# Chunk transposes by DVE blocks and SBUF transfers, second norm on ACT, in a gated recurrence with a binary FFN

## The chip, the cores and the metric

The kernel runs on one core of a Trainium2 chip. The core has five engines that run side by side, each through its own queue in order: PE (matrix products), DVE (element-wise work and statistics), ACT (activation functions), POOL (a slower element-wise engine) and SP, which here only issues DMA transfers. They meet through semaphores. The metric is the device time of the program in microseconds (us).

## The reference

The input x has 2 sequences of 4096 tokens with 256 features. A gated linear recurrence with a tanh state of 64 runs over the tokens, its result is projected and added to x, and a LayerNorm follows; then an FFN with weights reduced to a sign and a scale per row, exact Gelu, hidden width 1024, and a second LayerNorm:

```
u = x @ W_in + b_in
g = sigmoid(x @ W_gate + b_gate)
h_t = tanh(h_prev @ A + u_t @ Bm)
y_t = h_t @ C.T + u_t @ D.T
y_t = g_t * y_t + (1.0 - g_t) * x_t
x   = layernorm(x + (ys @ W_out + b_out + x))
h   = gelu(x @ binarize(w1).T + b1)
x   = layernorm(x + (h @ binarize(w2).T + b2))
```

Everything is float32. Where one operand of a product is a sign, the other is written as a sum of two parts in a faster product format (`fp32r`): `hi`, the rounded value, and `lo`, the rest. Two products give nearly the float32 result.

## The kernel before

**Tiles.** The sequences are cut into 64 segments each, which the recurrence advances together, 128 columns a step (with a warm-up that makes the segments independent). The rest of the work goes by 16 chunks of 512 tokens. A chunk lives in two layouts: tokens on partitions (`x1`, a tile `xn` of 128 partitions x 4 blocks x 256 features) for the norms, and features on partitions (`hi`/`lo`, named `xhi`/`xlo`, 128 x 2 x 512) as the input of the first FFN product.

**A chunk's way.** `load` fetches the states and inputs of the recurrence (`hu`) and the rows of x (`xn`). `mix` makes y's first term on PE (`ps_y`) and `d` on DVE; `mix_end` applies the gate (two DVE operations, L382 and L385). `project` multiplies by W_out on PE (`ps_z`), adds the residual on DVE (L406) and starts the first norm's statistics (`bs_a`, `mv_a`, `rs_a`; the power is taken on POOL). `shift` and `norm` apply that norm on ACT (`nm_a`, then four activations, L279). `turn` transposes x1 with eight PE transposes into PSUM (`ps_t`, L423), makes `xhi` on ACT (L431) and `xlo` on DVE (L433). `rest` adds the row b2 on POOL (L355). Four groups g of `up`, `low` and `down` do the FFN: `up` multiplies (`ps_h`, L451), applies Gelu twice on ACT (L458) and rounds (`hhi`, L467); `low` makes `hlo` on DVE (L474); `down` multiplies by w2 (`ps_o`, L490), and after its last group `scale` takes the sum out of PSUM (`o`, L506). `add` adds the residual (L512), `stats` starts the second norm (`bs_b`, `mv_b`, `rs_b`), and `store` applies it, on DVE unless told otherwise (four operations, L281; on ACT it first makes `nm_b` on DVE, L271), and writes the chunk out on SP's queue.

**Order.** PE, ACT, DVE and POOL follow an order written out by hand: the order in which the Python code calls the pieces is the order of each engine's queue. SP's queue is ordered by the scheduler. In the main loop, iteration c works on several chunks at once: `up`, `low`, `down` 0 and 1 of chunk c, `down` 2 and 3, `add`, `stats` and `store` of chunk c - 1, `norm` and `turn` of chunk c + 1, `mix` and `project` of chunk c + 2. `step` puts one step of the recurrence between them (`ps_s` on PE, a tanh on ACT, L158) as long as any are left, and gate products (`ps_g`, L313) of a late chunk go in as well. So one iteration of the loop before is, in order:

```
up 0, low 0, step, down 2 (c-1), load (c+3), shift, norm (c+1), mix (c+2)
up 1, step, down 3 (c-1), add, stats (c-1), gate
turn (c+1), low 1, rest (c+1)
up 2, low 2, store (c-1), step, down 0, project 0 (c+2)
up 3, step, down 1, low 3, project 1 (c+2)
```

**Buffers.** `d` and `o` each have one buffer of 4 KB a partition, `xhi` and `xlo` two each. In PSUM the tag "m" (one buffer of two banks) serves `ps_y`, `ps_z` and `ps_t` in turn, and three single banks serve `ps_h` and `ps_g`.

Of the kernel before, what the change touches and what calls it, by code (L numbers as in the profile page):

```python
# [8 lines left out]
FP = mybir.dt.float32  # L9
FR = mybir.dt.float32r  # L10
# [6 lines left out]
P = 128  # L17
B, T, DM, S, H = 2, 4096, 256, 64, 1024
KD = DM // P
# [4 lines left out]
N = 512  # L24
# [3 lines left out]
TB = N // P  # L28
# [9 lines left out]
def gated_recurrence_then_binary_ffn(  # L38
# [16 lines left out]
    nc = tc.nc  # L55
# [3 lines left out]
    wk = ctx.enter_context(tc.tile_pool(name="work", bufs=2))  # L59
# [269 lines left out]
    class Chunk:  # L329


        def __init__(self, c, name, at=lambda a, c: a[c]):
            self.c, self.nm, self.at, self.xt = c, name, at, None

        def load_x(self):
            self.xt = xp.tile([P, KD, N], FP, tag="xt", name=f"xt_{self.nm}", bufs=XTB)
# [28 lines left out]
        def mix(self):  # L365

            nm, xt_ = self.nm, self.xt
            ps = p_m.tile([P, KD, N], FP, tag="m", name=f"ps_y{nm}")
            for m in range(KD):
                nc.tensor.matmul(  # L370
                    ps[:, m, :], cd[:, bass.ts(m, P)], self.hu, start=True, stop=True
                )
                if m < KD - 1:
                    yield
            self.add_row(self.xn, bo_r)
            self.d = wk.tile([P, KD, N], FP, tag="y", name=f"d{nm}", bufs=1)
            nc.vector.tensor_sub(self.d, ps, xt_)
            yield

# [38 lines left out]
        def turn(self, apart=False):  # L418
# [15 lines left out]
            self.h = {}  # L434
            yield

        def rest(self):

            self.add_row(self.x1, b2_r)
            yield  # L440

        def up(self, g, apart=False):
            nm = f"{self.nm}_{g}"
            h = wk.tile([P, 2, N], FP, tag="h", name=f"h{nm}")
            hi = wk.tile([P, 2, N], FR, tag="hhi", name=f"hhi{nm}", bufs=3)
            self.h[g] = h, hi
            for i in range(2):
                j = 2 * g + i
                ps = p_1.tile([P, N], FP, tag="h", name=f"ps_h{nm}_{i}")
                for n, (k, part) in enumerate((k, p) for p in (self.hi, self.lo) for k in range(KD)):  # L450
                    nc.tensor.matmul(  # L451
                        ps,
                        sg1[:, k, bass.ts(j, P)],
                        part[:, k, :],
                        start=n == 0,
                        stop=n == 2 * KD - 1,
                    )
                nc.scalar.activation(  # L458
                    h[:, i, :],
                    ps,  # L460
                    AF.Gelu,
                    bias=b1_c[:, j : j + 1],
                    scale=al1[:, j : j + 1],
                )
                if i == 1:
                    for part in range(2) if apart else [slice(0, 2)]:
                        nc.scalar.copy(hi[:, part, :], h[:, part, :])  # L467
                yield
# [167 lines left out]
    def do(i, what, *args, pace=5600):  # L636
        if not 0 <= i < len(ch):
            return
        if what == "load":
            need = WARM + (ch[i].c + 1) * SPC  # L640
            while done < need:
                next_steps()
            ch[i].load()
        elif what in ("load_x", "load_gate_x"):
            getattr(ch[i], what)()
        else:
            emit(what, getattr(ch[i], what)(*args), pace)
# [7 lines left out]
    with tc.manual_schedule(engines={ET.PE, ET.Activation, ET.DVE, ET.Pool}):  # L655
        waiting = []
        for c in range(FIRST + 1, FIRST + 6):
            load_xT(c)
        idle_products(7)
        emit("u", u_of_chunks(FIRST), 1 << 30)  # L660
        since = 0
        pairs = [(5, 6), (7, 8), (9, 10), (11, 12), (13, 14), (), (1, 2)]
        loads = [[10, 11], [12, 13], [14, 15, 0], [1, 2], [3], [], []]
        for n, pair in enumerate(pairs):
            before = 2 if n == 0 else 1
            parts(before, EARLY)
            if pair:
                emit("", u_of_chunks(*pair))
                if pair == (13, 14):
                    emit("", u_of_chunks(15, 0))  # L670
                emit("u", [None], EARLY)
            for c in loads[n]:
                load_xT(c)
            if n == 0:
                load_weights()
            if n == 3:
                halve_weights()
            if n >= 5:
                load_xT(n + 3)
            for i in range(7 - before):  # L680
                if 1 <= n < 5 and i == 0:
                    load_w(n - 1)
                if 2 <= n < 6 and i == 3:
                    prepare_w(n - 2)
                parts(1 if (n, i) != (6, 5) else 0, EARLY)
        assert done >= WARM + SPC, done
        emit("u", u_of_chunks(3), EARLY)
        for i in range(4):
            ch[i].xt = x_tiles[i]
        do(0, "mix", pace=850)  # L690
        do(0, "mix_end")
        parts(1, 600)
        assert done >= WARM + 2 * SPC, done
        do(1, "mix", pace=850)
        do(1, "mix_end")
        parts(1, 600)
        do(0, "project", 0, p_2, "o", pace=1700)
        do(0, "project", 1, pace=1700)
        assert done >= WARM + 3 * SPC, done
        do(2, "mix", pace=1700)  # L700
        do(0, "shift")
        do(1, "project", 0, p_2, "o", pace=1700)
        do(0, "norm")
        do(1, "project", 1, pace=1700)
        mixed = ch[2].mix_end()
        next(mixed)
        parts(2, 1700)
        while waiting:
            next_steps()
        waiting = None  # L710
        do(0, "turn", True)
        emit("", mean_w2())
        do(1, "norm", nc.vector)
        do(0, "rest")
        next(mixed)
        parts(2, 1700)
        for i in (4, 5):
            do(i, "load_x")
        end = len(ch) - 1
        parts_met = compare()  # L720
        since = -1 << 40
        late = gates(ch[10:], TB)
        for c in range(end):
            do(c + 6, "load_x")
            if c % 2 == 0:
                do(10 + c // 2, "load_gate_x")
            do(c, "up", 0)
            do(c, "low", 0)
            step()
            do(c - 1, "down", 2)  # L730
            do(c + 3, "load")
            if c > 0:
                do(c + 1, "shift")
                do(c + 1, "norm")
                do(c + 2, "mix")
                do(c + 2, "mix_end")
            do(c, "up", 1)
            step()
            do(c - 1, "down", 3)
            def add():  # L740
                do(c - 1, "add", range(TB), nc.gpsimd if c == end - 1 else nc.vector)
                if c < end - 1:
                    do(c - 1, "stats")

            if 1 <= c <= 12:
                add()
                emit("gate", (next(late, None) for _ in range(KD)))
            do(c + 1, "turn")
            do(c, "low", 1)
            if not 1 <= c <= 12:  # L750
                add()
            do(c + 1, "rest")
            do(c, "up", 2)
            do(c, "low", 2)
            if c == end - 1:
                do(c - 1, "stats")
            else:
                do(c - 1, "store")
            if c == end - 2:
                assert done == len(plan), done  # L760
                next(parts_met)
                next(parts_met)
            step()
            do(c, "down", 0)
            do(c + 2, "project", 0)
            do(c, "up", 3)
            step()
            do(c, "down", 1)
            do(c, "low", 3)
            if c == end - 1:  # L770
                do(c - 1, "store")
            do(c + 2, "project", 1)
            if c == end - 2:
                next(parts_met)
                next(parts_met)
        count()
        do(end, "up", 0)
        do(end, "low", 0)
        do(end - 1, "down", 2)
        do(end - 1, "down", 3)  # L780
        do(end, "up", 1)
        do(end - 1, "add")
        do(end - 1, "stats")
        do(end, "low", 1)
        do(end, "up", 2)
        do(end, "low", 2)
        do(end, "down", 0, True)
        do(end, "up", 3, True)
        do(end - 1, "store", range(TB), nc.scalar)
        do(end, "low", 3, True)  # L790
        do(end, "down", 1)
        do(end, "down_end")
# [64 lines left out]
```

## Time and profile before

| What | Value |
|---|---|
| Median of the runs | 451.27 us |
| Lowest and highest of three runs | 451.14 and 453.04 us |
| The profiled execution | 451.76 us, of it a span of 450.0 us |
| Transposes on PE, `ps_t` | 128 of 0.274 us each |
| `xlo` from PSUM on DVE | 15 of 1.219 us (and two halves) |
| The second norm on DVE, L281 | 58 of 0.695 us, four to a chunk |
| The first norm on ACT, L279 | 60 of 0.591 us, four to a chunk |
| `hu`, the transfers from SBUF to SBUF | 32 of 128 KB, 2.2 us from issue to landing |

The span is the time from the first to the last instruction that the profile shows. Mean durations of pipelined instructions overlap: eight transposes of 0.274 us take less than eight times that. The up products of the first iteration begin at 87.2 us, those of the last chunk end some 15 us before the span's end; the iterations between are nearly equal, and what is read of one of them holds for the others.

### The profile page before, as it was taken

How to read it: one execution, taken by the hardware profiler on the slowest of the kernel's cores; microseconds unless marked ns; L12 is line 12 of the kernel's file. 1: busy time of each engine (PE TensorE's matmuls, PEld its weight loads, DVE VectorE, ACT ScalarE, POOL GpSimd, SP SyncE). 2: the span in 40 equal slices, each digit the busy share in tenths (PEclk: the TensorE clock that was granted, in tenths of full speed). 3: DMA queues.
4: the chain of work that ended last, by engine and by line, in shares of the span. 5: the costliest groups of instructions: out<-in, count | busy, mean ns of one | idle time of the engine just before them, and what ended most of it. 6: DMA issues, size and time to landing. Idle time of an engine off the chain costs nothing.

```text
span 450.0 us, 6729 instructions
## 1 busy us (share of the span) xinstructions
PE 438.2 (97%) x2506; PEld 355.6 (79%) x2506; DVE 357.4 (79%) x597; ACT 259.9 (58%) x424; POOL 177.6 (39%) x177
## 2 busy tenths in 40 slices
PE   8999999999999999999999999999999999999992
PEld 5665766788888888887979797979788888897982
DVE  0245927967979797989898889899898989887774
ACT  2443541585656574847474747566666656565771
POOL 1001300643545454545445454545454545433413
PEclk9999999999999999999999999999999999999997
DMA  8997824221133313331331313111202020201013
GB/s 298 306 320 289 290 67 134 69 86 23 48 108 104 108 58 106 105 106 58 105 106 61 105 60 105 61 58 50 70 20 87 1 93 1 93 1 48 1 47 101
DMA packets 14838, 44.51 MB, mean 99 GB/s; under 512 B 2000, under 2 KB 3024, under 8 KB 14800
## 3 DMA queue, kind: packets, MB, share of 16 engines
q1 hardware_dynamic: 14224, 43.65, 29.2%
q8 instruction: 22, 0.36, 0.4%
q10 hardware_dynamic: 576, 0.37, 0.3%
q14 instruction: 16, 0.13, 0.1%
HBM read 31.43 MB, written 8.39 MB: 88 GB/s over the span
## 4 chain that ended last, share of the span: by engine, by line
PE 86%; DVE 6%; DMA 3%; ACT 3%; issue 1%; POOL 1%; SPq 0%; POOLq 0%; DVEq 0%
PE ps_h L451 24%; PE ps_o L490 23%; PE ps_z L395 12%; PE ps_g L313 11%; PE ps_y L370 6%; PE ps_s L157 5%; PE ps_u L131 3%; PE ps_t L423 3%; DMA xt<-in_xT 3%; DVE hlo L474 1%; ACT xn L279 1%; ACT h L458 1%; DVE xn L281 1%; DVE bs_a L256 1%; ACT hhi L467 1%
## 5 line engine op out<-in xcount | busy, mean ns | idle before, releaser
L458 ACT ACTIVATE h<-ps_h,bias_c,al 128x512 f32<-128x512 f32 x128 | 97.4, 776 | 86.3 <-PE ps_h L451 80.3
L490 PE MATMUL ps_o<-sg,hhi 128*128 128x256 f32 x496 | 121.3, 285 | 0.0
L490 PE MATMUL ps_o<-sg,hlo 128*128 128x256 f32 x496 | 117.9, 279 | 0.1
L474 DVE TENSOR_TENSOR hlo<-h,hhi 128x1024 fp32r<-128x1024 f32 (+1 forms) x65 | 83.7, 1305 | 23.1 <-ACT hhi L467 23.0
L490 PEld LDWEIGHTS ps_o<-sg,hlo 128*128 128x128 f32 x496 | 93.5, 188 | 1.1 <-DVE hlo L474 0.3
L490 PEld LDWEIGHTS ps_o<-sg,hhi 128*128 128x128 f32 x496 | 93.5, 189 | 0.8
L451 PE MATMUL ps_h<-xhi,sg 128*128 128x512 f32 x256 | 91.8, 440 | 0.0
L355 POOL TENSOR_TENSOR xn<-xn,bo_r 128x256 f32<-128x256 f32 x64 | 65.4, 1052 | 48.4 <-DMA xn<-in_x 48.4
L451 PE MATMUL ps_h<-xlo,sg 128*128 128x512 f32 x256 | 80.1, 394 | 0.2
L355 POOL TENSOR_TENSOR xn<-xn,b_r 128x256 f32<-128x256 f32 x64 | 70.8, 1134 | 2.0 <-PE ps_t L423 2.0
L467 ACT CAST hhi<-h 128x1024 fp32r<-128x1024 f32 (+1 forms) x65 | 67.3, 1037 | 2.0
L313 PE MATMUL ps_g<-xt,w_gate 128*128 128x384 f32 (+3 forms) x208 | 66.3, 430 | 0.2 <-DMA xt<-in_xT 0.2
L266 POOL TENSOR_TENSOR rs_a<-rs_a,neg_half 128x4 f32<-128x4 f32 x16 | 17.2, 1075 | 121.3 <-DVE rs_a L265 96.6
L395 PE MATMUL ps_z<-w_out,tg 128*128 128x256 f32 x256 | 60.7, 380 | 0.0
L158 ACT ACTIVATE st<-ps_s 64x128 f32<-64x128 f32 x112 | 30.1, 269 | 47.6 <-PE ps_s L157 47.1
L451 PEld LDWEIGHTS ps_h<-xlo,sg 128*128 128x128 f32 x256 | 48.1, 188 | 11.8 <-DVE xlo L433 0.9
L451 PEld LDWEIGHTS ps_h<-xhi,sg 128*128 128x128 f32 x256 | 46.6, 189 | 13.4 <-issue 6.2
L157 PEld LDWEIGHTS ps_s<-st,wab 128*128 128x128 f32 x224 | 38.5, 188 | 22.2 <-ACT st L158 10.0
L266 POOL TENSOR_TENSOR rs_b<-rs_b,neg_half 128x4 f32<-128x4 f32 (+1 forms) x17 | 19.2, 1132 | 87.9 <-PE ps_s L157 49.9
L395 PEld LDWEIGHTS ps_z<-w_out,tg 128*128 128x128 f32 x256 | 46.1, 189 | 5.1
L279 ACT ACTIVATE xn<-xn,nm_a,rs_a 128x256 f32<-128x256 f32 x60 | 31.2, 591 | 26.5 <-DVE nm_a L271 26.5
L157 PE MATMUL ps_s<-st,wab 128*128 128x128 f32 x224 | 43.9, 278 | 0.1
(73 smaller groups left out, 483.5 us busy)
## 6 DMA issues: line engine op xcount, KB each, us to landing
xt<-in_xT SPq DMA_DIRECT2D x35, 512.0 KB, 4.2
xn<-in_x SPq DMA_DIRECT2D x16, 512.0 KB, 3.4
out_y<-xn SPq DMA_DIRECT2D x15, 512.0 KB, 2.6
hu<-st SPq DMA_DIRECT2D x32, 128.0 KB, 2.2
w1t<-in_w1T SPq DMA_DIRECT2D x2, 512.0 KB, 5.6
w1n<-in_w SPq DMA_DIRECT2D x2, 512.0 KB, 6.3
w2t<-in_w2T SPq DMA_DIRECT2D x2, 512.0 KB, 4.7
xt<-in_xT SPq DMA_DIRECT2D x2, 256.0 KB, 3.4
```

The source lines that it names most:

```text
L157: nc.tensor.matmul(p_h, ab, st[:, j].rearrange("p b k -> p (b k)"), start=True, stop=True)
L158: nc.scalar.activation(h_of[:, j + 1].rearrange("p b k -> p (b k)"), p_h[TOP, :], AF.Tanh)
L266: nc.gpsimd.tensor_tensor(rs, rs, neg_half[:, cut], ALU.pow)
L279: nc.scalar.activation(r, r, AF.Identity, bias=self.sh[:, i : i + 1], scale=rs)
L313: nc.tensor.matmul(ps[:, cut], w_gate[:, k, bass.ts(m, P)], xt_[:, k, cut], start=k == 0 and i == 0, stop=k == KD - 1, skip_group_check=True,)
L355: nc.gpsimd.tensor_tensor(r[:, i, :], r[:, i, :], row, ALU.add)
L395: nc.tensor.matmul(self.ps_z[:, i, :], self.y[:, k, bass.ts(i, P)], w_out[:, k, :], start=k == 0, stop=k == KD - 1,)
L451: nc.tensor.matmul(ps, sg1[:, k, bass.ts(j, P)], part[:, k, :], start=n == 0, stop=n == 2 * KD - 1,)
L458: nc.scalar.activation(h[:, i, :], ps, AF.Gelu, bias=b1_c[:, j : j + 1], scale=al1[:, j : j + 1],)
L467: nc.scalar.copy(hi[:, part, :], h[:, part, :])
L474: nc.vector.tensor_sub(lo[:, i, :], h[:, i, :], hi[:, i, :].bitcast(FP))
L490: nc.tensor.matmul(ps[:, i, :], part[:, j % 2, bass.ts(tb, P)], sg2[:, j, :], start=j == 0 and part is self.h[j // 2][0] and first, stop=j ...
```

## The change

From chunk 2 on, `turn` is replaced by two new pieces. `blocks`, called in iteration c behind `mix_end` of chunk c + 2, transposes x1 of chunk c + 1 on DVE in 32x32 blocks into a new tile `xb` (one buffer) and issues sixteen transfers on SP's queue, each 32 partitions x 2 rows x 512 B, from `xb` to `xlo`. The features then lie on their partitions, with the tokens of a chunk in the order (part a of 32, block i, place c). `split`, called for chunk c + 1 inside `up` 3 of chunk c behind its second Gelu, copies `xlo` to `xhi` on ACT with rounding and subtracts on DVE, in place. Gelu's output is written with the token order put right again, so that everything after it is as before. Chunk 0 and chunk 1 keep `turn`, the latter in iteration 0.

The second norm (`store` of chunk c - 1, c = 1 to 13) is applied on ACT instead of DVE. `xb` takes 4 KB a partition; `d` shares the buffer of `o`.

```diff
@@ -331,6 +331,7 @@
 
         def __init__(self, c, name, at=lambda a, c: a[c]):
             self.c, self.nm, self.at, self.xt = c, name, at, None
+            self.far = False
 
         def load_x(self):
             self.xt = xp.tile([P, KD, N], FP, tag="xt", name=f"xt_{self.nm}", bufs=XTB)
@@ -373,7 +374,7 @@
                 if m < KD - 1:
                     yield
             self.add_row(self.xn, bo_r)
-            self.d = wk.tile([P, KD, N], FP, tag="y", name=f"d{nm}", bufs=1)
+            self.d = wk.tile([P, KD, N], FP, tag="o", name=f"d{nm}", bufs=1)
             nc.vector.tensor_sub(self.d, ps, xt_)
             yield
 
@@ -434,12 +435,36 @@
             self.h = {}
             yield
 
+        def blocks(self):
+
+
+            nm, Q = self.nm, P // 32
+            xb = wk.tile([P, DM // 32, TB, 32], FP, tag="xb", name=f"xb{nm}", bufs=1)
+            nc.vector.transpose(
+                out=xb, in_=self.x1.rearrange("p i (b r) -> p b i r", r=32)
+            )
+            self.lo = wk.tile([P, KD, N], FR, tag="xlo", name=f"xlo{nm}")
+            for a in range(Q):
+                for q in range(Q):
+                    nc.sync.dma_start(
+                        out=self.lo.bitcast(FP)[bass.ts(q, 32), :, bass.ts(a, P)],
+                        in_=xb[bass.ts(a, 32), q :: Q, :, :].rearrange("p k i c -> p k (i c)"),
+                    )
+            yield
+
+        def split(self):
+            self.hi = wk.tile([P, KD, N], FR, tag="xhi", name=f"xhi{self.nm}")
+            nc.scalar.copy(self.hi, self.lo.bitcast(FP))
+            nc.vector.tensor_sub(self.lo, self.lo.bitcast(FP), self.hi.bitcast(FP))
+            self.h = {}
+            self.far = True
+
         def rest(self):
 
             self.add_row(self.x1, b2_r)
             yield
 
-        def up(self, g, apart=False):
+        def up(self, g, apart=False, between=None):
             nm = f"{self.nm}_{g}"
             h = wk.tile([P, 2, N], FP, tag="h", name=f"h{nm}")
             hi = wk.tile([P, 2, N], FR, tag="hhi", name=f"hhi{nm}", bufs=3)
@@ -455,14 +480,19 @@
                         start=n == 0,
                         stop=n == 2 * KD - 1,
                     )
+                to = h[:, i, :]
+                if self.far:
+                    to = to.rearrange("p (i a c) -> p a i c", a=P // 32, c=32)
                 nc.scalar.activation(
-                    h[:, i, :],
-                    ps,
+                    to,
+                    ps.rearrange("p (a i c) -> p a i c", a=P // 32, c=32) if self.far else ps,
                     AF.Gelu,
                     bias=b1_c[:, j : j + 1],
                     scale=al1[:, j : j + 1],
                 )
                 if i == 1:
+                    if between is not None:
+                        between()
                     for part in range(2) if apart else [slice(0, 2)]:
                         nc.scalar.copy(hi[:, part, :], h[:, part, :])
                 yield
@@ -734,6 +764,7 @@
                 do(c + 1, "norm")
                 do(c + 2, "mix")
                 do(c + 2, "mix_end")
+                do(c + 1, "blocks")
             do(c, "up", 1)
             step()
             do(c - 1, "down", 3)
@@ -745,7 +776,8 @@
             if 1 <= c <= 12:
                 add()
                 emit("gate", (next(late, None) for _ in range(KD)))
-            do(c + 1, "turn")
+            if c == 0:
+                do(1, "turn")
             do(c, "low", 1)
             if not 1 <= c <= 12:
                 add()
@@ -755,7 +787,7 @@
             if c == end - 1:
                 do(c - 1, "stats")
             else:
-                do(c - 1, "store")
+                do(c - 1, "store", range(TB), nc.scalar)
             if c == end - 2:
                 assert done == len(plan), done
                 next(parts_met)
@@ -763,7 +795,7 @@
             step()
             do(c, "down", 0)
             do(c + 2, "project", 0)
-            do(c, "up", 3)
+            do(c, "up", 3, False, ch[c + 1].split if c > 0 else None)
             step()
             do(c, "down", 1)
             do(c, "low", 3)
```

## The prediction

> **What bounds the kernel now.** I read the page's busy times first, then a table of the steady stretch cut at one recurring instruction, then the waits inside it, then the timelines of DVE and ACT over one period.
>
> ```profile
> PE 438.2 (97%) x2506; PEld 355.6 (79%) x2506; DVE 357.4 (79%) x597; ACT 259.9 (58%) x424; POOL 177.6 (39%) x177
> ...
> 276.86:300.27 23.41, 23.41 (x138) 19.66 (x138) 20.94 (x35) 14.60 (x23) 11.29 (x11) 1.00 0.25 79
> ...
> sum 279.49, PE 279.49 PEld 234.38 DVE 251.24 ACT 173.50 POOL 134.76; mean PE 23.29 PEld 19.53 DVE 20.94 ACT 14.46 POOL 11.23
> ```
>
> The stretches run from one last mixing instruction (L385) to the next, c = 1 to 13: twelve periods, 279.49 us. PE is busy through every one (23.41 of 23.41), so PE sets the period. DVE has only 2.4 us to spare.
>
> ```profile
> 276.86 1.65 DVE L385 SCALAR_TENSOR_TENSOR tg<-xt,d 128x1024 f32<-128x1024 f32 x1
> 278.43 1.21 DVE L506 TENSOR_TENSOR o<-ps_o,al_r 128x1024 f32<-128x1024 f32 x1
> 279.68 1.23 DVE L512 TENSOR_TENSOR xn<-xn,o 128x1024 f32<-128x1024 f32 x1
> 280.94 1.41 DVE L256 BATCH_NORM_STATS2 bs_b<-xn 128x6 f32<-128x256 f32 x4
> ...
> 282.73 1.22 DVE L433 TENSOR_TENSOR xlo<-ps_t,xhi 128x1024 fp32r<-128x1024 f32 x1
> 283.87 2.88 DVE L474 TENSOR_TENSOR hlo<-h,hhi 128x1024 fp32r<-128x1024 f32 x2
> 286.67 2.65 DVE L281 TENSOR_SCALAR xn<-xn,mv_b,rs_b 128x256 f32<-128x256 f32 x4
> 290.25 1.23 DVE L474 TENSOR_TENSOR hlo<-h,hhi 128x1024 fp32r<-128x1024 f32 x1 [0.93 <-ACT hhi L467]
> ...
> 297.02 0.69 DVE L271 SCALAR_TENSOR_TENSOR nm_a<-mv_a,rs_a 128x4 f32<-128x4 f32 x1
> ```
>
> The second norm's apply (L281, 2.65 us) sits where DVE would otherwise wait for ACT; nothing waits for it but the store. ACT in the same period:
>
> ```profile
> 276.32 1.43 ACT L458 ACTIVATE h<-ps_h,bias_c,al 128x512 f32<-128x512 f32 x2
> 277.79 1.05 ACT L467 CAST hhi<-h 128x1024 fp32r<-128x1024 f32 x1
> ...
> 297.74 2.08 ACT L279 ACTIVATE xn<-xn,nm_a,rs_a 128x256 f32<-128x256 f32 x4 [1.73 <-DVE nm_a L271]
> 299.73 0.77 ACT L458 ACTIVATE h<-ps_h,bias_c,al 128x512 f32<-128x512 f32 x1
> ```
>
> A norm on ACT costs 1.99 us from its start to the next instruction (299.73 - 297.74). It starts 0.03 us after its shift nm_a ends: ACT follows DVE at once, and everything behind it on ACT waits too.
>
> [...] The blocks are 32 KB; the nearest thing in this trace, hu (128 KB, SBUF to SBUF), lands 2.2 us after issue and holds SP for 0.488 us. [...] a pair of hlo takes 2.80 us beside POOL's row additions, 2.51 without (at 96.77).
>
> **The change, part by part.**
>
> PE. Eight transposes go, for chunks 2 to 15. At 279.76 the first starts, at 280.55 the first product behind them: 0.79 us. The products that follow start 0.12 us later behind a gate product than behind transposes (0.66 against 0.54 us for the first two), so 0.67 us a period; chunk 15's set, with its waits, is 2.46 us (412.48 to 414.94). PE alone would need 23.41 - 0.67 = 22.7 us.
>
> DVE. The starts of one period (276.86 to 300.27) give 21.23 us of work and 2.18 of waiting (0.93, 0.65, 0.60). Away: the apply 2.65, xlo from PSUM 1.14. New: the block transpose, not in the trace; [...] I take 1.25. xlo from SBUF, 1.22 (as an hlo alone). nm_b, 0.73 (nm_a beside POOL's additions; 0.16 without them). Work: 21.23 - 2.65 - 1.14 + 1.25 + 1.22 + 0.73 = 20.64 us. That alone would fit under PE.
>
> The waits are what matters. The new order on DVE is: transpose, o, add, statistics, hlo1, hlo2, nm_b, xlo, hlo3. On ACT: hhi2, the four applies, the step's tanh, two Gelus of group 3, xhi, hhi3. The applies wait for nm_b; xhi stands behind them on ACT; xlo, the very next instruction on DVE, waits for xhi. So DVE must stand still from the end of nm_b to the end of xhi, whatever else is ready: 1.99 for the applies, 0.17 for the tanh (94.43 to 94.60 back to back), 1.47 for two Gelus (276.32 to 277.79), 1.05 for xhi (as hhi, also SBUF to SBUF), 0.06 for two handovers: 4.74 us. Before, DVE waited 2.18 in all, and the store hung on nothing. Nor can the other three waits cover it: hlo3, L407 and hlo0 come after, when their inputs are there. The period becomes 20.64 + 4.74 = 25.4 us.
>
> PE feels it twice: the up products of the next chunk wait for xlo, and the step behind up 3 waits for the tanh that stands behind the applies. From d's start to nm_b's end is 13.2 us, applies and tanh 2.2, step to next up 0 3.6 (264.75 to 268.34), up 0 to d 6.0 (244.82 to 250.86): 25.0 us, a second ring about as long.
>
> SP and the transfers. Sixteen DMAs a chunk behind the transpose, moved in SP's queue ahead of the gate x, the store, the next hu and xn. The issue time of a 32-partition, two-row transfer is unknown: 0.33 us (x loads) to 0.8, a little over one and a half hu; I take hu's 0.49. Then 16 x 0.49 = 7.8, and the last lands 1.7 later: 9.5 us after the transpose. The ring asks for xhi's start 7.83 (o to nm_b) + 3.66 (ACT up to xhi) = 11.5 us after it. Hidden, with 2 us over; from 0.6 us an issue it isn't. [...] The store behind them becomes ready when the applies end, 2 us after the sixteenth is out; xn for c + 3 waits for that store (2.6 us) and lands (3.4) well before its row addition.
>
> Priced at nothing: the Gelu's permuted write (same elements, PSUM read in order; if it were 0.1 us dearer, two of them are in the ring, 2.6 us in all); d in o's buffer (both on DVE, in order); the freed PSUM turn (no waits of PE on it now).
>
> Sum, against the profiled execution (451.76 us, its span 450.0, so 1.76 around it; the median of the runs is 0.49 below). Chunks 1 to 13: 12 x 25.4 = 304.8 against 279.49: +25.3. From the last mix (392.43) to chunk 14's xlo products (405.49) is 13.06; by the same sum 10.24 on DVE, 4.57 on ACT (no tanh), 1.22 xlo: 16.0, +3.0. Chunk 15 has no mix to hide its transfers: from chunk 14's xlo, 6.0 to nm_a, 2.1 norm, 1.25 transpose, 7.9 issue, 1.7 landing, 1.05 xhi, 1.25 xlo = 21.3 against 17.67 (405.49 to 423.16): +3.6. After that nothing changes. +31.9: span 481.9, time 483.7, by the median 483; I take 482, as some starts overlap by hundredths.
>
> **Rivals.**
> The ring, as summed: 482; transpose and small terms at their low ends give a period of 24.7 and 472, the transpose at twice gives 26.5 and 498. 66%.
> Transfers become the bound: at 0.7 us an issue the period grows by 1.5 us; 13 x 1.5 and 3.4 for chunk 15 put it at 505, at 0.8 at 527. For it: sixteen small transfers in one queue, an untested shape. Against: 0.33 to 0.49 for every SP issue seen. 17%.
> A lighter ring: the applies begin earlier than I think, because DVE runs faster once POOL and it collide less; a period of 23.5 to 24.7: 457 to 472. 9%.
> The other side: PE stays the bound. It needs a ring under 22.7, 2.7 us shorter than my sum, that is, nearly no wait at xlo. Then 12 x 0.67 and 2.46 and some at chunk 14 are saved: 451 - 11 = 440. For it: PE is the bound now, DVE's work falls by 0.6, ACT is only 62% busy in the period. Against: the order of the two queues, which leaves DVE nothing to do in that wait. 6%. The last 2% is a cancellation within 0.5% (about what a measurement can tell from no change).
>
> Chances: faster 0.06, same 0.02, slower 0.92. The range 464 to 505 takes in the ring's own 472 to 498, half of the lighter ring and the milder transfers.
>
> **What would show it.** Right: the xlo line on DVE waits some 4.7 us for ACT xhi in each period; period 25.4; PE waits on xlo or on the step's tanh, 2 us or more; the four applies end before the Gelus of group 3 start. Wrong: ACT xhi waits for the DMA (issue above 0.6 us), a transpose over 1.6 us, PE without gaps, or DVE's work under 18 us.

## The result and the profile after

The change makes the kernel slower: 497.99 us (median of four runs, 497.38 to 503.48) against 451.31 us, a ratio of 1.1052 with a 95% interval of 1.0969 to 1.1134. The profiled execution took 497.7 us with a span of 495.9, so the span grew by 45.9 us. The prediction said 482 us, slower, range 464 to 505.

In the kernel after, the lines are: block transpose L443, block transfers L449, `xhi` L457, `xlo` L458, d L378, mix L383 and L386, the step's tanh L158, Gelu L486, `hhi` L497, `hlo` L504, o L536, add L542, both norms on ACT L279.

The busy times of the page, and its row for the block transfers (count, size, us from issue to landing):

```profile
PE 446.2 (90%) x2394; PEld 354.1 (71%) x2394; DVE 341.0 (69%) x572; ACT 283.0 (57%) x476; POOL 166.0 (33%) x177
...
xlo<-xb SPq DMA_DIRECT2D x224, 32.0 KB, 1.9
```

PE does 112 transposes less and is busy for only 90% of the span. Its busy time in us has still grown, from 438.2 to 446.2: for parts of this run the clock granted to PE is half of full speed (0.50 from 309.90 to 312.03; PEclk in the table below is a period's mean, 0.93 where that stretch lies), and the same products take longer (a `ps_o` product with `hhi` 0.296 us on average, before 0.285). DVE is less busy too. No engine is full any more: the kernel runs at the pace of a ring, a chain of waits that goes through several queues and meets itself again one period later. The table of stretches, cut as before at one recurring mix instruction (L386, c = 1 to 13):

```profile
core 0: us, PE busy (x) PEld busy (x) DVE busy (x) ACT busy (x) POOL busy (x), PEclk, DMA share, GB/s
...
296.50:322.67 26.17, 24.39 (x130) 20.21 (x130) 19.61 (x33) 16.45 (x27) 10.19 (x11) 0.93 0.30 91
...
sum 314.51, PE 285.56 PEld 232.68 DVE 233.98 ACT 194.60 POOL 121.91; mean PE 23.80 PEld 19.39 DVE 19.50 ACT 16.22 POOL 10.16
```

The twelve periods sum to 314.51 us against 279.49: +35.0 of the 45.9. DVE is busy for 19.5 us of each 26.2. Where the rest goes is in the waits (waiting engine and line, what it waited for, us in total, times, longest):

```profile
DVE xlo L458 <- ACT xhi L457: 77.5, 14, 6.0
ACT xn L279 <- DVE nm_b L271: 55.2, 14, 6.0
...
PEld ps_s L157 <- ACT st L158: 36.3, 39, 3.1
```

`xlo` on DVE waits 5.5 us for ACT's `xhi`, on average over 14 chunks (77.5 / 14). In the period shown of before, `xlo` waited for nothing. One period on DVE, in the timeline (start, duration, operation, and in brackets the idle time ahead of it and what ended it):

```profile
296.50 1.65 DVE L386 SCALAR_TENSOR_TENSOR tg<-xt,d 128x1024 f32<-128x1024 f32 x1
298.07 1.23 DVE L443 STREAM_TRANSPOSE xb<-xn 128x1024 f32<-128x1024 f32 x1
299.24 1.18 DVE L536 TENSOR_TENSOR o<-ps_o,al_r 128x1024 f32<-128x1024 f32 x1
...
303.51 2.35 DVE L504 TENSOR_TENSOR hlo<-h,hhi 128x1024 fp32r<-128x1024 f32 x2
305.79 0.70 DVE L271 SCALAR_TENSOR_TENSOR nm_b<-mv_b,rs_b 128x4 f32<-128x4 f32 x1
312.14 1.23 DVE L458 TENSOR_TENSOR xlo<-xlo,xhi 128x1024 fp32r<-128x1024 f32 x1 [5.65 <-ACT xhi L457]
...
319.42 0.69 DVE L271 SCALAR_TENSOR_TENSOR nm_a<-mv_a,rs_a 128x4 f32<-128x4 f32 x1
```

ACT in the same stretch:

```profile
306.52 2.08 ACT L279 ACTIVATE xn<-xn,nm_b,rs_b 128x256 f32<-128x256 f32 x4 [3.22 <-DVE nm_b L271]
308.50 0.25 ACT L158 ACTIVATE st<-ps_s 64x128 f32<-64x128 f32 x1
308.66 1.43 ACT L486 ACTIVATE h<-ps_h,bias_c,al 128x512 f32<-128x512 f32 x2
311.06 1.04 ACT L457 CAST xhi<-xlo 128x1024 fp32r<-128x1024 f32 x1 [0.97 <-DMA xlo<-xb]
```

and SP's queue:

```profile
299.33 10.29 SPq L449 DMA_DIRECT2D xlo<-xb  x16
309.74 0.52 SPq L557 DMA_DIRECT2D out_y<-xn  x1
```

Read together: DVE ends nm_b at 306.49, ACT starts the applies at once, tanh and two Gelus follow, and ACT would be ready for `xhi` at 310.09. There it waits 0.97 us more, for the last of the sixteen transfers, which hold SP for 10.29 us, 0.643 each. Two chains end in `xhi`, then, the one through ACT's queue and the one through SP's, and SP's is the longer by about 1 us.

The rest of the 45.9 us is behind the last period. From the last mix (427.29) to chunk 14's first `xlo` products (444.20) it is 16.91 us, before 13.06: +3.85. From there to chunk 15's (467.98) it is 23.78, before 17.67: +6.1. What remains is 27.92 against 26.84: +1.1. In the last stretch ACT and PE show what they wait for:

```profile
465.62 1.04 ACT L457 CAST xhi<-xlo 128x1024 fp32r<-128x1024 f32 x1 [6.29 <-DMA xlo<-xb]
```

```profile
466.72 1.22 PE L476 MATMUL ps_h<-xhi,sg 128*128 128x512 f32 x2 [6.25 <-ACT xhi L457]
```

Chunk 15 has nothing left to hide its transfers behind, so PE stands for 6.25 us. The sum is 35.0 + 3.85 + 6.1 + 1.1 = 46.05. The stretch ahead of the first of these periods is 0.16 us shorter than before (112.78 against 112.94), which leaves the 45.9.

### The profile page after: what moved, and what is told of

Its sections match the earlier page's. It is cut to its first block, busy times and chain, and to the rows that moved or that the text cites. A ratio compares the mean times of both kernels' runs of the same rounds, so it can differ in the third digit from the quotient of the medians.

```text
span 495.9 us, 6834 instructions
## 1 busy us (share of the span) xinstructions
PE 446.2 (90%) x2394; PEld 354.1 (71%) x2394; DVE 341.0 (69%) x572; ACT 283.0 (57%) x476; POOL 166.0 (33%) x177
## 4 chain that ended last, share of the span: by engine, by line
PE 45%; DVE 24%; SPq 16%; ACT 7%; issue 4%; DMA 2%; POOL 1%; POOLq 0%; ACTq 0%; DVEq 0%
SPq L449 16%; PE ps_o L520 10%; PE ps_h L476 9%; PE ps_g L313 8%; PE ps_z L396 4%; PE ps_s L157 4%; PE ps_y L371 4%; DVE hlo L504 4%; PE ps_u L131 3%; DVE tg L386 3%; ACT xn L279 3%; DVE d L383 3%; DVE d L378 2%; DMA xlo<-xb 2%; DVE xb L443 2%
## 5 line engine op out<-in xcount | busy, mean ns | idle before, releaser
L520 PE MATMUL ps_o<-sg,hhi 128*128 128x256 f32 x496 | 128.0, 296 | 2.3 <-DVE o L536 2.3
L520 PE MATMUL ps_o<-sg,hlo 128*128 128x256 f32 x496 | 123.8, 288 | 0.1
L486 ACT ACTIVATE h<-ps_h,bias_c,al 128x512 f32<-128x512 f32 x128 | 95.7, 771 | 39.3 <-PE ps_h L476 35.2
L476 PE MATMUL ps_h<-xhi,sg 128*128 128x512 f32 x256 | 97.6, 463 | 12.5 <-ACT xhi L457 12.5
L520 PEld LDWEIGHTS ps_o<-sg,hhi 128*128 128x128 f32 x496 | 98.8, 199 | 5.0 <-DVE o L536 4.2
L520 PEld LDWEIGHTS ps_o<-sg,hlo 128*128 128x128 f32 x496 | 98.5, 199 | 1.1 <-DVE hlo L504 0.3
L504 DVE TENSOR_TENSOR hlo<-h,hhi 128x1024 fp32r<-128x1024 f32 (+1 forms) x65 | 78.0, 1217 | 13.2 <-ACT hhi L497 13.1
L266 POOL TENSOR_TENSOR rs_a<-rs_a,neg_half 128x4 f32<-128x4 f32 x16 | 22.2, 1390 | 159.4 <-DVE rs_a L265 151.3
L458 DVE TENSOR_TENSOR xlo<-xlo,xhi 128x1024 fp32r<-128x1024 f32 x14 | 17.2, 1226 | 77.5 <-ACT xhi L457 77.5
L497 ACT CAST hhi<-h 128x1024 fp32r<-128x1024 f32 (+1 forms) x65 | 67.2, 1036 | 1.6
L157 PE MATMUL ps_s<-st,wab 128*128 128x128 f32 x224 | 45.9, 287 | 22.2 <-ACT st L158 22.1
L266 POOL TENSOR_TENSOR rs_b<-rs_b,neg_half 128x4 f32<-128x4 f32 (+1 forms) x17 | 28.1, 1655 | 106.8 <-DVE rs_b L265 106.7
L279 ACT ACTIVATE xn<-xn,nm_b,rs_b 128x256 f32<-128x256 f32 x58 | 30.1, 590 | 55.2 <-DVE nm_b L271 55.2
L158 ACT ACTIVATE st<-ps_s 64x128 f32<-64x128 f32 x112 | 29.8, 266 | 46.7 <-PE ps_s L157 46.2
```

What stands on the lines that cost most here:

```text
L157: nc.tensor.matmul(p_h, ab, st[:, j].rearrange("p b k -> p (b k)"), start=True, stop=True)
L266: nc.gpsimd.tensor_tensor(rs, rs, neg_half[:, cut], ALU.pow)
L279: nc.scalar.activation(r, r, AF.Identity, bias=self.sh[:, i : i + 1], scale=rs)
L476: nc.tensor.matmul(ps, sg1[:, k, bass.ts(j, P)], part[:, k, :], start=n == 0, stop=n == 2 * KD - 1,)
L486: nc.scalar.activation(to, ps.rearrange("p (a i c) -> p a i c", a=P // 32, c=32) if self.far else ps, AF.Gelu, bias=b1_c[:, j : j + 1], sc ...
L504: nc.vector.tensor_sub(lo[:, i, :], h[:, i, :], hi[:, i, :].bitcast(FP))
```

## The experiments

Two theories of the 35 us in the periods. *Two rings*: the store's ring (nm_b, four applies, tanh, Gelus, `xhi`, `xlo`, on two in-order queues) is about 25.2 us long and the transfers' ring (transpose, 16 issues, landing, `xhi`, `xlo`, and round to the next transpose) 26.2; the longer sets the period, and taking one away leaves the other. *One ring*: only one of the two counts, and the other change costs nothing.

### The store back on DVE

```diff
-                do(c - 1, "store", range(TB), nc.scalar)
+                do(c - 1, "store")
```

> The change with the second norm's apply back on DVE; the transposes and the sixteen transfers stay. Theory of two rings of nearly equal length (transfers: transpose, sixteen issues of 0.64 us, landing, xhi, xlo, about 26.2 us; store on ACT: about 25.2 us): the outer one is untouched, and the apply falls into DVE's wait for xhi, so the period stays at 26 and the time at 494 to 499. Rival, as the prediction had it (the store's ring alone): the period falls to 24 or less, 455 to 463.

Measured: 499.62 us (498.91 to 500.12), ratio 1.1045 (1.1013 to 1.1077). Giving DVE its apply back saves nothing. The wait has moved, as ACT's timeline shows:

```profile
312.62 1.04 ACT L457 CAST xhi<-xlo 128x1024 fp32r<-128x1024 f32 x1 [3.19 <-DMA xlo<-xb]
```

`xhi` waits 3.19 us for the transfers instead of 0.97, since ACT is there sooner. The twelve periods average 26.4 us. So the transfers alone are enough for the whole loss of the change.

### Four transfers instead of sixteen

Each transfer now covers all 128 partitions and one part of the tokens. The features then reach partitions that are not theirs: the kernel leaves out the interchange of the blocks between partitions, and keeps the bytes.

```diff
             for a in range(Q):
-                for q in range(Q):
-                    nc.sync.dma_start(
-                        out=self.lo.bitcast(FP)[bass.ts(q, 32), :, bass.ts(a, P)],
-                        in_=xb[bass.ts(a, 32), q :: Q, :, :].rearrange("p k i c -> p k (i c)"),
-                    )
+                nc.sync.dma_start(
+                    out=self.lo.bitcast(FP)[:, :, bass.ts(a, P)],
+                    in_=xb[:, a::Q, :, :].rearrange("p k i c -> p k (i c)"),
+                )
```

> The change with four transfers of 128 partitions each chunk in place of sixteen of 32, the same bytes in the same rows of 512 B; the features land on the wrong partitions, so the blocks are not carried to their place and the values differ, the work on the engines doesn't. Two rings: the store's ring of 25.2 us remains, 12 x 1.0 less, and chunk 15 gets back some 7.5 us: 475 to 482. Transfers alone: PE becomes the bound again, 440 to 447. Store alone: only chunk 15 gains, 488 to 492.

Measured: 478.10 us (476.26 to 480.44), ratio 1.0556 (1.0519 to 1.0594), as the two rings have it. The four issues, in SP's queue, and the wait that is left, on DVE:

```profile
319.24 2.66 SPq L448 DMA_DIRECT2D xlo<-xb  x4
```

```profile
306.44 1.23 DVE L457 TENSOR_TENSOR xlo<-xlo,xhi 128x1024 fp32r<-128x1024 f32 x1 [4.58 <-ACT xhi L456]
```

Four times the bytes in one transfer hold SP no longer: 2.66 / 4 = 0.67 us against 0.64. The issue is paid per transfer here. With the transfers out of the way the store's ring shows itself: DVE stands 4.58 us, and the twelve periods sum to 304.29 us (112.81 to 417.10), 25.4 on average. They are not alike, as two rows of the table of stretches show:

```profile
265.96:292.32 26.36, 24.43 (x130) 20.20 (x129) 19.74 (x33) 16.33 (x27) 9.13 (x10) 0.94 0.27 90
292.32:316.41 24.09, 22.16 (x125) 18.10 (x124) 19.10 (x32) 15.66 (x26) 9.18 (x10) 1.00 0.31 99
```

Six periods have PE at its full clock throughout and average 24.51 us. Five have a clock of 0.93 or 0.94 and take 26.08 to 26.83; in each of these, and in none of the six, DVE also waits 1.07 to 1.15 us for PE's `ps_z`:

```profile
283.56 1.22 DVE L407 SCALAR_TENSOR_TENSOR xn<-xn,ps_z 128x1024 f32<-128x1024 f32 x1 [1.11 <-PE ps_z L396]
```

The twelfth (25.05, clock 0.93) has its slow stretch at its very end. So the store's ring is 24.5 us by itself, and PE's slow stretches lengthen it. They don't lengthen the change's own period: there the periods with a clock of 1.00 average 26.4 us and those with 0.93 or 0.94 average 26.1.

### Both

```diff
-                do(c - 1, "store", range(TB), nc.scalar)
+                do(c - 1, "store")
```

together with the four transfers of the run before.

> Both edits together: apply on DVE and four transfers (the features on the wrong partitions, as there). Two rings: both are cut, PE or DVE (22.7 and 22.6 us of work) is the bound, 440 to 449. Each rival alone expects here what it expects with its own edit: store alone 445 to 455, transfers alone 440 to 447.

Measured: 444.82 us (444.77 to 447.68), ratio 0.9855 (0.9812 to 0.9897). With neither ring PE is the bound again, and its eight transposes fewer count: periods of 22.48 us, PE busy through all of it, against 23.41. DVE's part of the change, the block transpose and `xlo` from SBUF, costs nothing in this place.

### Only the second norm on ACT, nothing else of the change

The kernel before with one line of the change:

```diff
-                do(c - 1, "store")
+                do(c - 1, "store", range(TB), nc.scalar)
```

> The kernel before with one edit: the second norm's apply on ACT; the transposes stay on PE. Two rings: the tanh of the recurrence still stands behind the applies, so the ring d to nm_b, applies, tanh, step, up 0 (24.9 us) holds while steps are left, and the wait at hlo3 (24.0 us) after that: 460 to 470. Rival (the store hurts only through xlo, which here is made earlier): 450 to 454.

Measured: 474.33 us (474.01 to 474.87), ratio 1.0484 (1.0456 to 1.0513): more than I expected of it, +22.2 us. DVE waits in its queue for ACT in the same way, though there are no transfers; here the operation behind nm_b is `hlo` of group 3. PE waits for the tanh behind the applies. DVE, then PE:

```profile
303.97 1.22 DVE L474 TENSOR_TENSOR hlo<-h,hhi 128x1024 fp32r<-128x1024 f32 x1 [4.71 <-ACT hhi L467]
```

```profile
301.58 0.49 PE L157 MATMUL ps_s<-st,wab 128*128 128x128 f32 x2 [1.38 <-ACT st L158]
```

The twelve periods average 25.04 us. With this run the four corners are: before 452, store on ACT 474, transfers 500, both 498. The two losses don't add; the larger stands.

### The tanh ahead of the applies

In the run above DVE and PE both wait behind the applies. Which of the two sets the 25.04?

```diff
-            else:
-                do(c - 1, "store", range(TB), nc.scalar)
             if c == end - 2:
...
             step()
+            if c == end - 1:
+                do(c - 1, "stats")
+            else:
+                do(c - 1, "store", range(TB), nc.scalar)
```

> Before, with the second norm applied on ACT (the run at 474 us) and the step's tanh issued ahead of the four applies instead of behind them. If the 22 us of that run came through the tanh (PE's step product waits for it) alone: back to 450 to 455. If they came through DVE's wait for hhi of group 3, which stands behind the applies on ACT, alone: 472 to 476, nothing changes. If both rings are about as long, as the prediction has it for the change (25.4 and 25.0): DVE's work of 19.3 us and a wait of 4.7 us make 24.0 us a period, 12 x 1.0 less: 461 to 467.

Measured: 469.83 us (469.38 to 471.52), ratio 1.0412 (1.0378 to 1.0446). None of the three numbers: between "both rings" and "DVE's wait alone". PE's step product (`ps_s`) no longer waits for the tanh: its weight loads do so for 9.9 us in the whole run, as in the kernel before (10.0), where in the run above they did for 28.5. DVE goes on waiting:

```profile
300.13 1.22 DVE L474 TENSOR_TENSOR hlo<-h,hhi 128x1024 fp32r<-128x1024 f32 x1 [4.55 <-ACT hhi L467]
...
306.44 0.70 DVE L271 SCALAR_TENSOR_TENSOR nm_a<-mv_a,rs_a 128x4 f32<-128x4 f32 x1 [0.91 <-POOL rs_a L266]
```

The period is 24.57 us. My sum had left out the second wait, 0.91 us for POOL's power; with it 19.3 + 4.55 + 0.91 = 24.8. So DVE's wait behind ACT is what costs, some 18 of the 22 us, and the tanh is a ring only 0.5 us longer that lies over it.

### The same work in another order

The transpose moves one DVE operation ahead, and the second norm's shift and applies move behind `xhi` and `xlo`. All sixteen transfers stay.

```diff
-                do(c + 2, "mix_end")
+                mixed = ch[c + 2].mix_end() if c + 2 <= end else iter(())
+                next(mixed, None)
                 do(c + 1, "blocks")
+                next(mixed, None)
...
-            else:
-                do(c - 1, "store", range(TB), nc.scalar)
...
             do(c, "down", 1)
+            if c < end - 1:
+                do(c - 1, "store", range(TB), nc.scalar)
             do(c, "low", 3)
```

> The whole change, with two moves in the order and nothing else: the block transpose stands one DVE operation earlier (before L386 instead of behind it, 1.57 us), and the applies of the second norm on ACT, with their nm_b on DVE, stand behind xhi and xlo instead of ahead of them. Still 16 transfers of 32 partitions. Two rings: the store's ring is gone, the transfers' ring (26.2 us as measured in the change) loses 1.57 and becomes 24.6; 12 x 1.6 = 19 less than the change's 498, and chunk 15's transfers stay: 479 (474 to 484), with xhi on ACT still waiting for the last transfer. ACT's order alone (the store's ring is all): about 455. Neither ring, a loss from the work itself wherever it stands: 495 or more.

Measured: 464.93 us (464.29 to 466.37), ratio 1.0303 (1.0271 to 1.0336): 33 us below the change with the same instructions, and 9 below my lowest number. DVE, then ACT:

```profile
298.80 0.16 DVE L271 SCALAR_TENSOR_TENSOR nm_a<-mv_a,rs_a 128x4 f32<-128x4 f32 x1
...
301.26 1.24 DVE L443 STREAM_TRANSPOSE xb<-xn 128x1024 f32<-128x1024 f32 x1
302.43 1.69 DVE L386 SCALAR_TENSOR_TENSOR tg<-xt,d 128x1024 f32<-128x1024 f32 x1
```

```profile
314.24 1.04 ACT L457 CAST xhi<-xlo 128x1024 fp32r<-128x1024 f32 x1 [1.83 <-DMA xlo<-xb]
```

From the transpose's start to `xhi` it is 12.98 us (314.24 - 301.26), in the change 12.99 (311.06 - 298.07): the transfers' stretch is what it was, and still the bound. The other part of the ring, from `xlo` to the next transpose, fell from 12.10 us (312.14 to 324.24) to 9.46 (291.80 to 301.26). Of the 2.64 us the moved transpose is 1.57; the rest I had not counted. Most of it is nm_a, which takes 0.16 us instead of 0.69. In the change POOL's row additions run beside it (from 318.81, nm_a at 319.42); here the store of c - 1 leaves later, so the rows that follow it into its buffer land later and POOL adds them from 302.30 on. The periods average 23.57 us, 2.6 below the change; 12 x 2.64 = 31.7 of the 33.

### The reordered change, with the blocks carried over memory outside SBUF

One transfer writes `xb`, 512 KB, to a tile in the device's memory; four read it back with the blocks on their partitions. The order is that of the run above.

```diff
+    dr = ctx.enter_context(tc.tile_pool(name="dram", bufs=2, space=bass.MemoryType.DRAM))
...
-            for a in range(Q):
-                for q in range(Q):
-                    nc.sync.dma_start(
-                        out=self.lo.bitcast(FP)[bass.ts(q, 32), :, bass.ts(a, P)],
-                        in_=xb[bass.ts(a, 32), q :: Q, :, :].rearrange("p k i c -> p k (i c)"),
-                    )
+            far = dr.tile([P, DM // 32, TB, 32], FP, tag="far", name=f"far{nm}", bufs=2)
+            nc.sync.dma_start(out=far, in_=xb)
+            for q in range(Q):
+                nc.sync.dma_start(
+                    out=self.lo.bitcast(FP)[bass.ts(q, 32)].rearrange("r k (a n) -> r k a n", a=Q),
+                    in_=far.rearrange("(a r) b i c -> r b a (i c)", a=Q)[:, q::Q],
+                )
```

> As the run with the moved transpose and applies, but the blocks go through memory outside the chip's SBUF: one transfer writes the transposed tile (512 KB), four read it back in the other order, so 5 issues instead of 16. Two rings: 5 issues take about 2.7 us; if write and read land within about 2.5 us each, xhi comes 3 to 4 us before it is asked for, PE alone sets the period (22.5 us, as in the run with both edits): 443 (438 to 449), below before. Transfers cost by the byte or the read back is slow (over 8 us for both): the ring stays over 24 us and the time over 470.

Measured: 442.78 us (441.61 to 443.06), ratio 0.9796 (0.9768 to 0.9824). It beats both kernels. SP's queue, then ACT, then a period in the table of stretches:

```profile
294.47 0.33 SPq L449 DMA_DIRECT2D far<-xb  x1
297.13 2.60 SPq L451 DMA_DIRECT2D xlo<-far  x4
```

```profile
304.57 1.04 ACT L459 CAST xhi<-xlo 128x1024 fp32r<-128x1024 f32 x1
```

```profile
294.37:316.85 22.48, 22.48 (x130) 18.79 (x129) 18.47 (x33) 16.34 (x27) 10.26 (x10) 1.00 0.32 106
```

The reads are issued when the write has landed, 2.66 us after its issue, and the last is out at 299.73: 5.3 us from the write's issue, where the sixteen took 10.3. `xhi` has no wait in brackets. DVE still stands 2.83 us for `xhi` in this period, and that costs nothing: PE is busy for the whole 22.48 us, and ACT's applies of the second norm, the same 2.08 us as in the change, cost nothing behind `xlo` either. At chunk 15, where nothing covers the transfers, `xhi` waits 2.22 us for them instead of 6.29.

### The change with the store on DVE and the blocks over memory

The first experiment with the transfers of the last one, in the change's order.

> The change with the second norm's apply back on DVE (the run at 499.6 us, transfers' ring alone) and the 16 transfers replaced by one write and four reads through memory outside SBUF, in the same place of SP's queue. Cost by the number of transfers: PE sets the period again, 445 (440 to 450), as the run with four transfers and the apply on DVE. Cost by the bytes, or two landings in a row as long as 16 issues: 475 or more, with xhi waiting for the transfers.

Measured: 455.85 us (454.69 to 456.81), ratio 1.0086 (1.0052 to 1.0119): neither number. The two landings are not the reason in a late period, which on DVE reads:

```profile
311.09 3.07 DVE L282 TENSOR_SCALAR xn<-xn,mv_b,rs_b 128x256 f32<-128x256 f32 x4
314.08 1.21 DVE L460 TENSOR_TENSOR xlo<-xlo,xhi 128x1024 fp32r<-128x1024 f32 x1
```

`xlo` follows the apply with no wait. DVE itself is nearly full: busy for 21.73 us of the period of 22.88 (301.83 to 324.71), with 0.91 more in nm_a's wait for POOL. In each of the first eight periods `xlo` also waits, 0.25 to 0.96 us, for an `xhi` that waited for the transfers, and these eight average 23.5 us. With the apply on DVE there is no room left to take up such delays; with it on ACT, behind `xlo`, there is.

## Why the prediction was right, and where a term was off

The direction is right, and the time lies in the range, 16 us above the 482. The ring that was given most weight, 66%, is there but is not the one that sets the period: the transfers' ring lies over it, which stood as a rival with 17%, and "ACT xhi waits for the DMA", named as a sign of being wrong, came true. That 482 is still near is in part luck: the two rings happen to lie within 2 us of each other. The range took in the milder transfers on purpose.

**PE bound before; eight transposes fewer.** Right. The prediction had PE alone at 22.7 us a period; the two kernels without a ring have 22.48. In the period of before that the prediction shows, `ps_o` products (fp32r) start 0.115 us apart (15 from 288.49 to 290.21), `ps_z` products (float32, also 128x256) 0.19 (8 from 284.58 to 286.12).

**The costs on DVE.** Right: transpose 1.232 us (taken as 1.25, my estimate: the trace of before has no such operation), `xlo` from SBUF 1.23 (1.22), nm_b 0.70 (0.73). Only the work as a whole came out smaller, 26.17 - 5.65 - 0.59 = 19.93 us of starts without the waits against 20.64: the pair of `hlo` takes 2.35 us instead of 2.88 (2.80 from start to start, as the prediction counts it), since POOL no longer adds rows beside it: its additions start at 305.58 there, behind most of the pair (303.51 to 305.86), and at 283.96 before, 0.09 us behind the pair's start. POOL takes 2.37 us for the addition to `xn` of 128x1024 (chunk 15 of before, at 413.95) that takes DVE 1.23.

**DVE stands still behind ACT.** Right, and shown twice. With the transfers shortened, `xlo` waits 4.58 us (4.74 predicted). That the period is 25.4 there, as predicted, is luck: at full clock it is 24.51, which is the 19.93 of work above and 4.58 of waiting, and PE's slow stretches, which the prediction doesn't have, bring the average up. The kernel before with the apply alone on ACT loses 22 us, some 18 of them through the same kind of wait. The applies end before the Gelus of group 3 start (308.60 and 308.66), and PE's idle time is 26.21 - 23.80 = 2.4 us a period, as was named.

**The ring through the tanh, 25.0 us.** Right in kind: 25.04 us with the apply alone, and 24.57 when the tanh goes ahead.

**SP's issue, 0.49 us a block.** This term was mis-sized, and it is the step that failed. A block holds SP for 0.643 us from start to start (0.595 for the issue, the rest between two of them), so the sixteen take 10.29 instead of 7.8. The prediction took the issue time of `hu`, another shape, and argued that every SP issue seen took 0.33 to 0.49; some early ones were longer (an `hu` at 47.38 took 0.59). The prediction's own threshold, hidden up to 0.6 us, holds: at 0.643 `xhi` waits 0.97 us. So the transfers' ring, 26.2 us, lies over the store's. It is the rival "transfers become the bound" in a mild form: 12 periods at 26.21 instead of the predicted 25.4 make 9.7 us of the 14 by which the span was missed. The first two experiments show it, one with no gain from the store alone, the other with 20 us from fewer transfers.

**Behind the last period.** Chunk 14 took 16.91 us (16.0 predicted); 0.6 of the 0.9 is its first pair of up products, 1.26 us from the next (442.94 to 444.20) where it was 0.65 before: the next pair needs `xlo`, which DVE ends at 444.15. Chunk 15 took 23.78 (21.3 predicted), for SP's reason: its sixteen issues take 10.70 us, not 7.9. "After that nothing changes" was off by 1.1 us: from the first `xlo` products to the down products behind this group's up products it is 2.50 us (467.98 to 470.48), before 1.38 (423.16 to 424.54), as PE runs slowly at first behind its gap (granted clock 0.56 in these 2.50 us, 1.00 in the 1.38). Together 9.7 + 0.9 + 2.5 + 1.1 = 14.2, against 495.9 - 481.9 = 14.0.

**What an issue costs beside its transfer.** One issue takes a third of its transfer's time (0.64 us, landing 1.9 us after the issue), and sixteen issues in a row hold SP for 10.29 us, five times one landing.

Left open: whether moving only the transpose or only the store would do; the reordered runs have both. Issuing the blocks from two queues wasn't tried. Why PE's clock falls behind some gaps and not behind others of the same length isn't shown.

## What to carry to other kernels

When work is moved to another engine because that engine is less busy, look at what stands behind it in both in-order queues: the same four applies cost 22 us ahead of a value that DVE waits for, and nothing behind it. Count a transfer's issue per transfer and not per byte (0.64 us with 32 KB, 0.67 with 128 KB here), add the issues up along one queue, and ask whether anything covers the last landing; fewer and larger transfers can be worth a longer way (442.78 us with 5 issues over memory, 464.93 with 16 inside SBUF, in the same order). When two rings are nearly equal (26.2 and 24.5 us here), undoing the shorter one shows no gain, so take both away before you call either harmless.

## What the runs showed of the hardware that I had not expected

- One issue held SP for a median of 0.595 us with 32 KB on 32 partitions and for 0.62 with 128 KB on 128 (0.64 and 0.67 with the time between two). A plain write of 512 KB held SP for 0.33 us, and each of the four reads back, 128 KB with rows of 512 B, for 0.61. So the time doesn't follow the size; which property of the shape sets it, no run tells.
- Carrying 512 KB out to memory and back, 5 issues and two landings one after the other, was ready sooner than sixteen transfers inside SBUF. From the transpose's end to `xhi`, where ACT waited for it, it took 7.9 to 9.4 us in the last experiment (8.8 from 234.53 to 243.36), against 11.8 (299.30 to 311.06). In two early periods of the reordered run over memory it took 10.6 and 10.9.
- Behind gaps of PE of 2.40 us (ahead of 442.94) and of 6.25 us (ahead of 466.72), the pairs of up products from the first `xlo` pair on start 1.02 and 0.85 us apart, where later ones follow each other at 0.47 (448.53 to 449.00); the granted clock is 0.50 from 442.90 to 445.00 and from 466.70 to 468.50. In the run with both edits, a gap of 1.19 us at the same place (ahead of 398.19) was followed by a step of 0.57 us. The length of the gap alone doesn't decide: in the steady periods of the change, a gap of 1.78 us ahead of 308.81 is followed by down products 0.21 us apart instead of 0.11, with a granted clock of 0.50 from 309.90 to 312.03, while gaps of 1.77 us ahead of 125.07 and 177.45 lie in periods with a clock of 1.00.
- The same DVE operation, nm_a of 512 values, takes 0.16 us without and 0.69 us with POOL at work beside it: in the kernel before 0.16 at 250.12, where POOL stands idle from 249.54 to 250.64, and 0.68 at 273.62, where its row additions run from 273.01.
